# q and k of step 1 formed for two row tiles at once, and the memory pools of two layers laid over each other

## The chip, the core and the metric

The kernel runs on one core of a Trainium2 chip. The time is the device time of one execution in microseconds; before the change its median over three runs is 1698.4 us (1698.17 to 1698.85). The core has five engines that work side by side, each through its own queue in order: TensorE (PE in the profile, its weight loads PEld), VectorE (DVE), ScalarE (ACT), GpSimd (POOL) and SyncE (SP), which here only issues transfers.

## What is computed

The input is a feature matrix `x` (2708 x 256) and a weighted adjacency matrix `adj` (2708 x 2708). Layer 0 runs two steps of an attention with a nucleus cut beside a walk over the normalized adjacency:

```python
for n in range(2):
    q = Xa @ W1.T @ W2.T;  k = Xa @ W3.T          # 64 wide
    probs = softmax(q @ k.T)
    A = top_p(probs, 0.9), rows scaled to sum 1
    Xf = R @ Xf                                   # R = (adj + I) / row sums
    Xa = A @ Xa
    Z = Z + Xf @ U1[n].T + Xa @ U2[n].T
x = layernorm(x + layernorm(x + Z) * g + b)
```

Layer 1 is a graph attention with four heads over the nonzero entries of `adj`:

```python
Wh = x @ W[h]                                     # 64 wide, per head
e[i, j] = leaky_relu(s_i[i] + s_j[j], 0.2), masked by adj
out = layernorm(x + softmax_j(e) @ Wh)
```

## The kernel before

The 2708 rows are cut into 22 tiles: 16 of 128 rows and 6 of 110 (`rows`, `off`). Everything is float32.

**Layer 0** (`fast_layer0`, L454) has a setup that forms q and k of step 0 for groups of up to four tiles (L993 to L1014), and then two steps over the 22 row tiles (`step`, L947). For each row tile three kinds of work overlap:

- `search` (`scores`, then the cut): the logits of a tile three ahead (L594), their exponentials into `e` (L598), and then the nucleus threshold on DVE (L684 to L768), in step 1 with four passes of ACT (L619).
- `weigh` (L162): the attention. A tile's `e` is transposed by TensorE in six groups (L172), copied by ACT to `eT` (L178), and multiplied with the values (L187): `xe` in step 0, `ba` in step 1. After each group `between` runs one slot of other work.
- `walks` (L787): the product with the adjacency (L819), fed from SP's loads of `blk` (L93), a few matmuls for each slot.

When a walk or an attention of step 0 ends, a generator does the rest in pieces, one for each slot. `after_walk0` transposes the result by `turn` (L573, matmuls L577, copy L580) and multiplies it (`terms1`, L855); `after_attention0` (L841) transposes the attended tile `xa`, forms its q and k for step 1 in `project` (L559: four matmuls of 128 moving columns at L566, each shown as two records; copies L570 and L555 or L557), and multiplies it (`terms2`, L875), which yields `ba`. In step 1 `finish` adds the parts up on POOL (L894 to L896), does two layer norms by turns of DVE and POOL (L900 to L917), and calls `sources` (L136), which transposes the new `x` (L141), forms layer 1's values (L147, ACT to L157), stores them scaled to DRAM (`vd`, L160), and keeps three small factors (`sb`, `tj`, `s_src`).

Inside `with tc.manual_schedule` the order on PE, ACT, DVE and POOL is the order of the code. What lies outside it, layer 1 with it, is put between by a planner at build time, as its inputs and its memory come free by the planner's reckoning. SP's queue is ordered by the planner throughout.

At the end of layer 0 DVE sums up some flags of the cut, and a small matmul (L1078) adds them over the partitions.

**Layer 1** (`layer1`, L1090) goes over three groups of target tiles (8, 8 and 6) and, in each, over the 22 source tiles `j`. `targets` spreads `s_src` by transposes into `aux` (L1122) and ACT makes `r` of it (L1126). `neighbours` loads a block of `adjT` into `bar` (L1136; four buffers) and makes it a 0/1 mask (ACT L1137 and L1142; for diagonal blocks POOL L1140 and L1141 between). DVE makes four `pt` for each source tile (L1189, two buffers each), and TensorE sums them up: with the values `v` at L1197 and with `bj` for the denominators at L1204. Before the loop, ACT issues the loads of all 22 `v` (L1103) and POOL spreads all 22 `bj` (L1104). The function `settle` ends a group.

**Memory.** A pool takes a stretch of SBUF, pools lie one behind the other in the order in which they are opened, and layer 1's start again where layer 0's started. A tile of layer 1 can be written when the tiles of layer 0 on the same addresses have been read for the last time. The same holds for the eight banks of PSUM. Before the change layer 0's order is `w0`, `rowp`, `keep` (with `qT`, `yw`, `ba`, `rinv`, `kT1`), `heldp`, `sortp`, `finp`, `ep`, `wk`, `tpp`, `adjp`, and layer 1's is `keep1` (`v`, `bj`), `pp`, `rp`, `adjp1`, `pj`.

Of the kernel before, what the change touches and what calls it, by code (L numbers as in the profile page):

```python
# [8 lines left out]
F32 = mybir.dt.float32  # L9
# [5 lines left out]
PSUM = bass.MemoryType.PSUM  # L15

P = 128
# [21 lines left out]
HELD = 8  # L39
# [6 lines left out]
def kernel(  # L46
# [407 lines left out]
    def fast_layer0():  # L454

        l0 = ExitStack()
        w0 = l0.enter_context(tc.tile_pool(name="w0", bufs=1))
        rowp = l0.enter_context(tc.tile_pool(name="rowp", bufs=2))
        keep = l0.enter_context(tc.tile_pool(name="keep", bufs=1))
        HN = N // 2  # L460
        HT = NT // 2
        pieces = [(c, min(CHUNK, HN - c)) for c in range(0, HN, CHUNK)]
# [10 lines left out]
        heldp = l0.enter_context(tc.tile_pool(name="heldp", bufs=HELD))  # L473
# [40 lines left out]
        nc.gpsimd.memset(wants, 0.0)  # L514
        nc.gpsimd.memset(haves, 0.0)

        qT = keep.tile([P, N], F32, name="qT")
        yw = keep.tile([P, NT, D], F32, name="yw")
        ba = keep.tile([P, NT, D], F32, name="ba")
        rinv = keep.tile([P, NT], F32, name="rinv")  # L520

        dram = l0.enter_context(tc.tile_pool(name="dram", bufs=1, space=bass.MemoryType.DRAM))
        c1 = [dram.tile([P, D], F32, name=f"c1_{t}") for t in range(NT)]
        c2 = [dram.tile([P, D], F32, name=f"c2_{t}") for t in range(NT)]

        sortp = l0.enter_context(tc.tile_pool(name="sortp", bufs=1))
        finp = l0.enter_context(tc.tile_pool(name="finp", bufs=2))
        ep = l0.enter_context(tc.tile_pool(name="ep", bufs=3))
        wk = l0.enter_context(tc.tile_pool(name="wk", bufs=1))

        kT = [wk.tile([P, HN], F32, name="junk"), keep.tile([P, HN], F32, name="kT1")]
        tpp = l0.enter_context(tc.tile_pool(name="tpp", bufs=3))
        adjp = l0.enter_context(tc.tile_pool(name="adjp", bufs=3))
        ps_lg = l0.enter_context(tc.tile_pool(name="ps_lg", bufs=2, space=PSUM))
        ps_tr = l0.enter_context(tc.tile_pool(name="ps_tr", bufs=2, space=PSUM))
        ps_at = l0.enter_context(tc.tile_pool(name="ps_at", bufs=1, space=PSUM))
        ps_wk = l0.enter_context(tc.tile_pool(name="ps_wk", bufs=1, space=PSUM))


        tr = ps_tr.tile([P, 4, P], F32, name="tr")  # L540
# [15 lines left out]
            if low < m:  # L556
                copy(kT[s][DA:P, c0 + low - HN : c0 + m - HN], src[DA:P, low:m])  # L557

        def project(s, t, xT, copy_q, copy_k):  # L559

            m = rows[t]
            c0 = off[t]
            pj = ps_tr.tile([P, 4, P], F32, name="tr")
            for n, w in enumerate((wq, wk_sb)):
                for c in range(DC):
                    nc.tensor.matmul(  # L566
                        pj[:, n, :m], w[:, c].rearrange("p h e -> p (h e)"), xT[:, c, :m],
                        start=(c == 0), stop=(c == DC - 1),
                    )
            copy_q(qT[:, c0 : c0 + m], pj[:, 0, :m])  # L570
            keep_k(s, c0, m, pj[:, 1], copy_k)

        def turn(src, m, tp, copy):  # L573

            xT = rowp.tile([P, DC, P], F32, name="xT")
# [252 lines left out]
        def after_walk0(t, ac):  # L828
# [9 lines left out]
            terms1(t, xT)  # L838
            unfinished.remove(t)

        def after_attention0(t, xa):  # L841
            yield
            tp = ps_tr.tile([P, 4, P], F32, name="tr")
            xT = turn(xa, rows[t], tp, nc.scalar.copy)
            yield
            project(1, t, xT, nc.scalar.copy, nc.scalar.copy)
            yield
            terms2(t, xT)

        def terms1(t, xT):  # L850

            m = rows[t]
            cy = ps_tr.tile([P, 4, P], F32, name="tr").rearrange("p a b -> p (a b)")
            for c in range(DC):
                nc.tensor.matmul(  # L855
                    cy[:m], xT[:, c, :m], u_sb[:, 0, c].rearrange("p s e -> p (s e)"),
                    start=(c == 0), stop=(c == DC - 1),
                )
            r = rinv[:m, t : t + 1]
            cs = rowp.tile([P, D], F32, name="cs")  # L860
            nc.scalar.activation(cs[:m], cy[:m, 0:D], AF.Copy, scale=r)
            nc.scalar.activation(yw[:m, t, :], cy[:m, D : 2 * D], AF.Copy, scale=r)

            own = rowp.tile([P, D], F32, name="own")
            nc.gpsimd.tensor_scalar(own[:m], yw[:m, t, :], r, None, op0=ALU.mult)
            nc.gpsimd.tensor_add(cs[:m], cs[:m], own[:m])
            nc.gpsimd.tensor_add(cs[:m], cs[:m], xe[:m, t, 0:D])
            nc.gpsimd.dma_start(c1[t][:m], cs[:m])
# [78 lines left out]
        def step(s, cur, spend):  # L947
            for t in range(NT):
# [140 lines left out]

    def layer1():  # L1090
        l1 = ExitStack()
        keep = l1.enter_context(tc.tile_pool(name="keep1", bufs=1))
        pp = l1.enter_context(tc.tile_pool(name="pp", bufs=2))
        GT = 8
        spans = [list(range(g, min(g + GT, NT))) for g in range(0, NT, GT)]
        GW = GT * rows[0]


        v = [keep.tile([P, H, FO], F32, name=f"v{t}") for t in range(NT)]
        bj = [keep.tile([P, H, 32], F32, name=f"bj{t}") for t in range(NT)]  # L1100
        for t in range(NT):
            m = rows[t]
            nc.scalar.dma_start(v[t][:m].rearrange("p h o -> p (h o)"), vd[t][:m])  # L1103
# [4 lines left out]
        rp = l1.enter_context(tc.tile_pool(name="rp", bufs=2))  # L1108
        adjp = l1.enter_context(tc.tile_pool(name="adjp1", bufs=4))
        pj = l1.enter_context(tc.tile_pool(name="pj", bufs=2))  # L1110
        ps_v = l1.enter_context(tc.tile_pool(name="ps_v", bufs=1, space=PSUM))
        ps_u = l1.enter_context(tc.tile_pool(name="ps_u", bufs=2, space=PSUM))

        def targets(g):

# [55 lines left out]
        for g, span in enumerate(spans):  # L1171
# [6 lines left out]
            for j in range(NT):  # L1178
# [91 lines left out]
```

The softmax here doesn't subtract the row's maximum and nothing guards it: scores larger than these inputs give would overflow.

## Time and profile before

The profiled execution spans 1697.3 us. Busy time of the engines in stretches of it, in us:

| stretch | what runs | PE | DVE | ACT | POOL | clock of PE |
|---|---|---|---|---|---|---|
| 100 to 600 (500 us) | step 0 | 492.6 | 242.7 | 167.4 | 55.7 | 1.00 |
| 700 to 1200 (500 us) | step 1 | 494.8 | 460.1 | 331.2 | 206.7 | 1.00 |
| 1260 to 1310 (50 us) | end of layer 0, begin of layer 1 | 28.5 | 11.4 | 15.3 | 21.0 | 0.76 |
| 1400 to 1600 (200 us) | layer 1 | 196.4 | 174.2 | 71.6 | 44.6 | 1.00 |

A line of the groups gives line, engine, operation, output and input tiles and the number of instructions; then busy time, mean duration of one, and the idle time of the engine before them with what ended it. Matmuls of this engine are pipelined, so the durations of neighbours overlap, and the distance from start to start is shorter than a duration. A line of the timeline gives the start in us, the time that the merged run of instructions took, engine, line, operation and their number; a bracket tells how long the engine stood idle before it and who released it.

### The profile page before, as it was taken

Reading aid. Unit: us, or ns where it says so; the run is one execution under the profiler, and the core shown is the slowest. Engines: PE = TensorE matmul, PEld = TensorE weight load, DVE = VectorE, ACT = ScalarE, POOL = GpSimd, SP = SyncE. Lnnn points to the kernel's source line nnn. Section 1 sums busy time; section 2 is a strip of 40 time slices with the busy share of each in tenths; the row PEclk is TensorE's granted clock in tenths of the full one; section 3 lists DMA queues with packets and bytes.
Section 4 is the critical chain, followed back from the end, with each engine's and each line's share of the span. In section 5 each row is a group of like instructions: output and inputs, shape, how many; then the busy total and the mean of one; then the engine's idle time right before and its main releaser. Section 6 shows DMA issues by size and latency. Waiting matters only on the chain. (4 is left out here: it accounts for less than half of the span.)

```text
span 1697.3 us, 24178 instructions
## 1 busy us (share of the span) xinstructions
PE 1620.3 (95%) x8306; PEld 1064.8 (63%) x8306; DVE 1219.5 (72%) x3660; ACT 767.9 (45%) x1324; POOL 433.6 (26%) x915
## 2 busy tenths in 40 slices
PE   7999999999999999999999999999985999999895
PEld 4677777777767766777878788777773232322332
DVE  2954554556445029888899999998981989889886
ACT  1333333333333256566666767676723444243231
POOL 0310111111101033223344444453434200430312
PEclk9999999999999999999999999999996999999997
DMA  6211011101111133122223323322204323232231
GB/s 164 72 46 46 27 41 39 43 27 39 40 42 40 44 89 77 48 67 75 71 74 82 85 65 87 80 71 66 68 22 126 100 82 94 87 86 78 73 85 31
DMA packets 153873, 113.89 MB, mean 67 GB/s; under 512 B 39898, under 2 KB 144094, under 8 KB 153742
## 3 DMA queue, kind: packets, MB, share of 16 engines
q1 hardware_dynamic: 146248, 102.41, 22.7%
q0 software_dynamic: 2112, 5.55, 1.0%
q10 hardware_dynamic: 5382, 4.32, 0.9%
q8 instruction: 67, 1.10, 0.3%
q14 instruction: 64, 0.52, 0.1%
HBM read 101.16 MB, written 11.09 MB: 66 GB/s over the span
## 5 line engine op out<-in xcount | busy, mean ns | idle before, releaser
L1189 DVE SCALAR_TENSOR_TENSOR pt<-r,tj,bar 128x1024 f32<-128x1024 f32 (+3 forms) x264 | 297.0, 1187 | 49.8 <-ACT bar L1142 25.5
L619 ACT ACTIVATE junk<-e,minus,rth 128x2708 bf16<-128x2708 f32 (+1 forms) x88 | 233.0, 2648 | 36.1 <-POOL rth L651 35.3
L819 PE MATMUL walk<-xe,blk 128*128 128x257 f32 (+3 forms) x968 | 240.6, 382 | 0.0
L187 PE MATMUL att<-ba,eT 128*128 128x256 f32 (+3 forms) x968 | 234.4, 383 | 5.0 <-ACT eT L178 5.0
L187 PE MATMUL att<-xe,eT 128*128 128x256 f32 (+3 forms) x968 | 233.3, 381 | 4.3 <-ACT eT L178 4.3
L1197 PE MATMUL acc<-pt,v 128*64 128x512 f32 (+3 forms) x1056 | 230.5, 554 | 4.6 <-DVE pt L1189 4.6
L178 ACT COPY eT<-tr 128x512 f32<-128x512 f32 (+5 forms) x264 | 138.2, 538 | 203.3 <-PE tr L172 203.0
L819 PE MATMUL walk<-yw,blk 128*128 128x256 f32 (+3 forms) x968 | 228.0, 381 | 1.8 <-ACT xw L889 1.8
L699 DVE MAX8 cand<-e 128x8 f32<-128x170 f32 (+1 forms) x352 | 89.3, 324 | 171.5 <-ACT e L598 171.5
L819 PEld LDWEIGHTS walk<-xe,blk 128*128 128x128 f32 (+3 forms) x968 | 173.0, 186 | 53.1 <-issue 29.3
L819 PEld LDWEIGHTS walk<-yw,blk 128*128 128x128 f32 (+3 forms) x968 | 176.7, 186 | 41.6 <-issue 11.5
L187 PEld LDWEIGHTS att<-ba,eT 128*128 128x128 f32 (+3 forms) x968 | 171.9, 187 | 33.0 <-ACT eT L178 10.0
L187 PEld LDWEIGHTS att<-xe,eT 128*128 128x128 f32 (+3 forms) x968 | 170.8, 186 | 30.9 <-ACT eT L178 7.2
L598 ACT ACTIVATE e<-lg 128x1024 f32<-128x1024 f32 (+1 forms) x132 | 121.1, 922 | 132.3 <-PE lg L594 132.3
L1197 PEld LDWEIGHTS acc<-pt,v 128*64 128x64 f32 (+1 forms) x1056 | 73.7, 137 | 154.8 <-issue 111.9
L172 PE MATMUL tr<-ident,e 128*128 128x128 f32 (+3 forms) x968 | 140.5, 269 | 4.6 <-ACT xT L580 3.8
L172 PEld LDWEIGHTS tr<-ident,e 128*128 128x128 f32 (+3 forms) x968 | 115.0, 138 | 32.7 <-ACT xT L580 6.1
L1137 ACT ACTIVATE bar<-bar 128x1024 f32<-128x1024 f32 (+3 forms) x66 | 63.0, 956 | 146.0 <-DMA bar<-in_adjT_dram 110.1
L1204 PE MATMUL acc<-pt,bj 128*32 128x512 f32 (+3 forms) x1056 | 124.5, 549 | 0.0
L605 POOL TENSOR_TENSOR fact<-zp 128x1 f32<-128x1 f32 (+1 forms) x44 | 24.9, 566 | 329.2 <-ACT e L598 319.4
L699 DVE MAX8 cand<-scr 128x8 f32<-128x97 f32 (+1 forms) x616 | 101.9, 247 | 0.0
L832 DVE TENSOR_TENSOR xf<-walk,xe 128x257 f32<-128x257 f32 (+1 forms) x22 | 9.4, 427 | 117.4 <-PE walk L819 117.3
(199 smaller groups left out, 2022.1 us busy)
## 6 DMA issues: line engine op xcount, KB each, us to landing
blk<-in_adjT_dram SPq DMA_DIRECT2D x32, 704.0 KB
bar<-in_adjT_dram SPq DMA_DIRECT2D x32, 512.0 KB
blk<-in_adjT_dram SPq DMA_DIRECT2D x32, 330.0 KB
blk<-in_adjT_dram SPq DMA_DIRECT2D x32, 320.0 KB
blk<-in_adjT_dram SPq DMA_DIRECT2D x12, 605.0 KB
bar<-in_adjT_dram SPq DMA_DIRECT2D x12, 440.0 KB
bar<-in_adjT_dram SPq DMA_DIRECT2D x16, 330.0 KB
c<-cs POOLq DMA_DIRECT2D x32, 128.0 KB, 2.1
```

The costliest lines, as they stand in the source:

```text
L172: nc.tensor.transpose(tr[: rows[t], q, :m], e[:m, off[t] : off[t + 1]], ident[:m, :m])
L178: copy(eT[:k, : len(grp), :m], tr[:k, : len(grp), :m])
L187: nc.tensor.matmul(acc, eT[: rows[t], q, :m], value(t), start=(t == 0), stop=(t == NT - 1),)
L598: nc.scalar.activation(halves[:m, :, c0 : c0 + w], lg[:m, :, :w], AF.Exp, accum_out=zp[:m, n : n + 1],)
L605: nc.gpsimd.tensor_add(z, zp[:m, 0:1], zp[:m, 1:2])
L619: nc.scalar.activation(junk[:m], e[:m], func, scale=rth, bias=minus1[:m], accum_out=acc)
L699: nc.vector.max(cand[:, n, :], src[:m, n * size : min(N, (n + 1) * size)])
L819: nc.tensor.matmul(ac[:m, :w], blk[: rows[j], j - j0, :m], cur[: rows[j], j, 0:w], start=(j == 0), stop=(j == NT - 1),)
L1137: nc.scalar.activation(bar, bar, AF.Sign)
L1189: nc.vector.scalar_tensor_tensor(pt[:k, :gw], r[:k, h, :gw], tj[:k, j, h : h + 1], mask, op0=ALU.max, op1=ALU.mult,)
L1197: nc.tensor.matmul(acc[h // 2][c][q * FO : (q + 1) * FO, :w], v[j][:k, h - 1 + q, :], pts[h - 1 + q][:k, c0 : c0 + w], **at,)
L1204: nc.tensor.matmul(acc[2][c][h * 32 : (h + 1) * 32, :w], bj[j][:k, h, :], pts[h][:k, c0 : c0 + w], **at,)
```

## The change

Two things are changed. First, q and k of step 1 are formed once for two row tiles: the transposed tiles of a pair lie side by side in `xT2`, and `project` multiplies both with one set of matmuls of 256 moving columns (220 for the pairs of 110 rows). `xa` of step 0 then lies in `heldp`, and `own` has one buffer. Second, the pools of both layers are opened in an order in which each stretch of layer 1 lies over tiles of layer 0 that come free early enough for it; `v` and `bj` are allotted from the last tile to the first. With it the loads of `v` go from ACT's queue to SP's, and they and the copies of `bj` are written inside the first group's loop, one for each source tile.

```diff
     def fast_layer0():
 
         l0 = ExitStack()
-        w0 = l0.enter_context(tc.tile_pool(name="w0", bufs=1))
-        rowp = l0.enter_context(tc.tile_pool(name="rowp", bufs=2))
-        keep = l0.enter_context(tc.tile_pool(name="keep", bufs=1))
+
+        heldp, finp, rowp, w0, keep, sortp, adjp, ep, tpp, wk = (
+            l0.enter_context(tc.tile_pool(name=name, bufs=bufs))
+            for name, bufs in (
+                ("heldp", HELD), ("finp", 2), ("rowp", 2), ("w0", 1), ("keep", 1),
+                ("sortp", 1), ("adjp", 3), ("ep", 3), ("tpp", 3), ("wk", 1),
+            )
+        )
+        ps_lg, ps_wk, ps_at, ps_tr = (
+            l0.enter_context(tc.tile_pool(name=name, bufs=bufs, space=PSUM))
+            for name, bufs in (("ps_lg", 2), ("ps_wk", 1), ("ps_at", 1), ("ps_tr", 2))
+        )
...
-        qT = keep.tile([P, N], F32, name="qT")
         yw = keep.tile([P, NT, D], F32, name="yw")
         ba = keep.tile([P, NT, D], F32, name="ba")
         rinv = keep.tile([P, NT], F32, name="rinv")
+        qT = keep.tile([P, N], F32, name="qT")
...
-        def project(s, t, xT, copy_q, copy_k):
-
-            m = rows[t]
-            c0 = off[t]
-            pj = ps_tr.tile([P, 4, P], F32, name="tr")
-            for n, w in enumerate((wq, wk_sb)):
+        def project(s, c0, w, xT, copy_q, copy_k):
+
+            pj = ps_tr.tile([P, 4, P], F32, name="tr").rearrange("p (n a) b -> p n (a b)", n=2)
+            for n, wm in enumerate((wq, wk_sb)):
                 for c in range(DC):
                     nc.tensor.matmul(
-                        pj[:, n, :m], w[:, c].rearrange("p h e -> p (h e)"), xT[:, c, :m],
+                        pj[:, n, :w], wm[:, c].rearrange("p h e -> p (h e)"), xT[:, c, :w],
                         start=(c == 0), stop=(c == DC - 1),
                     )
-            copy_q(qT[:, c0 : c0 + m], pj[:, 0, :m])
-            keep_k(s, c0, m, pj[:, 1], copy_k)
+            copy_q(qT[:, c0 : c0 + w], pj[:, 0, :w])
+            keep_k(s, c0, w, pj[:, 1], copy_k)
...
+        pair = []
+
         def after_attention0(t, xa):
-            yield
+
+            m = rows[t]
+            yield
+            if t % 2 == 0:
+                pair[:] = [rowp.tile([P, DC, 2 * P], F32, name="xT2", bufs=1)]
+            both = pair[0]
+            xT = both[:, :, m * (t % 2) : m * (t % 2 + 1)]
             tp = ps_tr.tile([P, 4, P], F32, name="tr")
-            xT = turn(xa, rows[t], tp, nc.scalar.copy)
-            yield
-            project(1, t, xT, nc.scalar.copy, nc.scalar.copy)
-            yield
+            turn(xa, m, tp, nc.scalar.copy, xT)
+            yield
+            if t % 2:
+                project(1, off[t - 1], 2 * m, both, nc.scalar.copy, nc.scalar.copy)
+                yield
             terms2(t, xT)
...
-            own = rowp.tile([P, D], F32, name="own")
+            own = rowp.tile([P, D], F32, name="own", bufs=1)
...
-                        pool = heldp if s else rowp
-                        xa = pool.tile([P, D], F32, name=f"xa{s}")
+                        xa = heldp.tile([P, D], F32, name="xa1")
...
     def layer1():
         l1 = ExitStack()
-        keep = l1.enter_context(tc.tile_pool(name="keep1", bufs=1))
-        pp = l1.enter_context(tc.tile_pool(name="pp", bufs=2))
+
+        pp, keep, pj, adjp, rp = (
+            l1.enter_context(tc.tile_pool(name=name, bufs=bufs))
+            for name, bufs in (("pp", 2), ("keep1", 1), ("pj", 2), ("adjp1", 4), ("rp", 2))
+        )
+        ps_u = l1.enter_context(tc.tile_pool(name="ps_u", bufs=2, space=PSUM))
+        ps_v = l1.enter_context(tc.tile_pool(name="ps_v", bufs=1, space=PSUM))
...
-        v = [keep.tile([P, H, FO], F32, name=f"v{t}") for t in range(NT)]
-        bj = [keep.tile([P, H, 32], F32, name=f"bj{t}") for t in range(NT)]
-        for t in range(NT):
+        v, bj = {}, {}
+        for t in reversed(range(NT)):
+            v[t] = keep.tile([P, H, FO], F32, name=f"v{t}")
+            bj[t] = keep.tile([P, H, 32], F32, name=f"bj{t}")
+
+        def stationary(t):
             m = rows[t]
-            nc.scalar.dma_start(v[t][:m].rearrange("p h o -> p (h o)"), vd[t][:m])
+            nc.sync.dma_start(v[t][:m].rearrange("p h o -> p (h o)"), vd[t][:m])
             nc.gpsimd.tensor_copy(
                 bj[t][:m], sb[:m, t, :].unsqueeze(2).to_broadcast([m, H, 32])
             )
...
+                if g == 0:
+                    stationary(j)
                 mask = neighbours(g, j)
```

More of the change, by code (lines that the diff above doesn't have):

```diff
@@ L472, in fast_layer0 @@
         b_sb = w0.tile([P, D], F32, name="b_sb")
-        heldp = l0.enter_context(tc.tile_pool(name="heldp", bufs=HELD))
         tmp = heldp.tile([P, D], F32, name="xa1")
@@ L524, in fast_layer0 @@
         c2 = [dram.tile([P, D], F32, name=f"c2_{t}") for t in range(NT)]
[L526 to L529, printed above, removed]
         kT = [wk.tile([P, HN], F32, name="junk"), keep.tile([P, HN], F32, name="kT1")]
[L532 to L537, printed above, removed]
         tr = ps_tr.tile([P, 4, P], F32, name="tr")
@@ L557, in keep_k, with turn @@
                 copy(kT[s][DA:P, c0 + low - HN : c0 + m - HN], src[DA:P, low:m])
-        def project(s, t, xT, copy_q, copy_k):
-            m = rows[t]
-            c0 = off[t]
-            pj = ps_tr.tile([P, 4, P], F32, name="tr")
-            for n, w in enumerate((wq, wk_sb)):
+        def project(s, c0, w, xT, copy_q, copy_k):
+            pj = ps_tr.tile([P, 4, P], F32, name="tr").rearrange("p (n a) b -> p n (a b)", n=2)
+            for n, wm in enumerate((wq, wk_sb)):
                 for c in range(DC):
                     nc.tensor.matmul(
-                        pj[:, n, :m], w[:, c].rearrange("p h e -> p (h e)"), xT[:, c, :m],
+                        pj[:, n, :w], wm[:, c].rearrange("p h e -> p (h e)"), xT[:, c, :w],
                         start=(c == 0), stop=(c == DC - 1),
                     )
-            copy_q(qT[:, c0 : c0 + m], pj[:, 0, :m])
-            keep_k(s, c0, m, pj[:, 1], copy_k)
-        def turn(src, m, tp, copy):
-            xT = rowp.tile([P, DC, P], F32, name="xT")
+            copy_q(qT[:, c0 : c0 + w], pj[:, 0, :w])
+            keep_k(s, c0, w, pj[:, 1], copy_k)
+        def turn(src, m, tp, copy, xT=None):
+            if xT is None:
+                xT = rowp.tile([P, DC, P], F32, name="xT")
             for c in range(DC):
@@ L1106, in layer1 @@
             )
[L1108 to L1112, printed above, removed]
         def targets(g):
```

## The prediction

> **What bounds the kernel now.** I read the page's busy table and slices first, then the table by stage around the one weak slice, then the timeline there, and last the TensorE timeline inside step 1's projection. The chain that ended last is no help: it covers only the last 1.4 us.
>
> The busy table and the slices (each digit is a fortieth of the span, 42.4 us):
>
> ```profile
> PE 1620.3 (95%) x8306; PEld 1064.8 (63%) x8306; DVE 1219.5 (72%) x3660; ACT 767.9 (45%) x1324; POOL 433.6 (26%) x915
> PE   7999999999999999999999999999985999999895
> PEclk9999999999999999999999999999996999999997
> ```
>
> TensorE is the bound nearly everywhere. The one hole is where its row has 8 and 5 (about 1230 to 1315 us), the seam between the layers; the clock falls to 0.6 there. The table by stage cuts it finer:
>
> ```profile
> core 0: us, PE busy (x) PEld busy (x) DVE busy (x) ACT busy (x) POOL busy (x), PEclk, DMA share, GB/s
> 1279.70:1290.00 10.30, 4.91 (x21) 2.99 (x19) 3.13 (x9) 2.19 (x10) 7.97 (x14) 0.82 0.04 11
> 1290.00:1297.00 7.00, 6.13 (x23) 4.50 (x22) 0.33 (x1) 5.54 (x21) 0.00 (x0) 0.53 0.72 196
> 1297.00:1312.00 15.00, 3.17 (x17) 2.39 (x16) 1.31 (x2) 4.33 (x7) 6.46 (x25) 0.60 0.76 250
> 1312.00:1320.65 8.65, 8.62 (x32) 3.10 (x32) 8.65 (x7) 4.73 (x7) 6.12 (x6) 0.71 0.22 61
> 1320.65:1326.09 5.44, 5.44 (x36) 1.48 (x32) 5.44 (x5) 3.46 (x4) 1.79 (x2) 1.00 0.34 96
> ```
>
> The last attention matmul of layer 0 ends at 1279.7. Then comes the tail (residual sum, two layer norms and `sources` of the last tiles), an almost empty stretch, a slow first source tile of layer 1, and from 1320.65 the steady pace of 5.44 us per source tile. The timeline names the holder of the empty stretch:
>
> ```profile
> 1297.18 0.33 ACTq L1103 DMA_DIRECT2D v<-v  x1
> 1297.36 0.60 ACT L1126 ACTIVATE r<-aux 128x512 f32<-128x512 f32 x1
> 1297.55 11.04 ACTq L1103 DMA_DIRECT2D v<-v  x21
> 1308.63 1.09 ACT L1126 ACTIVATE r<-aux 128x512 f32<-128x512 f32 x2 [10.67 <-DMA v<-v]
> 1309.60 1.06 ACT L1142 ACTIVATE bar<-bar 128x1024 f32<-128x1024 f32 x1
> ```
>
> ACT issues all 22 loads of `v` while the rest of `r` and the first mask stand behind them in its queue; DVE's first `pt` starts at 1310.69 after 20.4 us of waiting for that mask, and TensorE's first `acc` at 1312.03.
>
> Inside step 0, the timeline of TensorE around one projection:
>
> ```profile
> 340.22 1.03 PE L819 MATMUL walk<-xe,blk 128*128 128x257 f32 x4
> 341.09 0.60 PE L172 MATMUL tr<-ident,e 128*128 128x128 f32 x4
> ...
> 343.26 0.61 PE L566 MATMUL tr<-xT,wq 128*128 128x128 f32 x4
> 343.71 0.61 PE L566 MATMUL tr<-xT,wk_sb 128*128 128x128 f32 x4
> 344.15 1.03 PE L819 MATMUL walk<-xe,blk 128*128 128x257 f32 x4
> ```
>
> Start to start is what counts here, not the duration: four records with 128 columns take 343.71 - 343.26 = 0.45 us, or 0.111 each; four with 257 take 341.09 - 340.22 = 0.87, or 0.218 each. The durations, 275 and 382 ns, overlap and would mislead.
>
> **What the Trainium skill says.** "TensorE: Matmul & The Clock Gate", section "Back-to-back issue gap", lets the gap of isolated matmuls grow with the moving columns plus a small constant, and warns that weight loads raise it at small widths. The trace shows proportion: 0.111 against 0.218, so no weight load shows at 128. The same page, "What's actually happening", says that an idle array falls to half rate and needs sustained work to recover; the trace agrees (clock 0.53 to 0.82 in the seam, four L147 records 2.10 us there against 1.05 at 1276). "DMA: Bandwidth & Descriptors", "Issuing engines are not separate DMA queues", says that the choice of issuing engine saves only sequencer time, usually small; here it is not small, 11.4 us of ACT. "GPSIMD Engine Reference", "Key points", says that GpSimd shares its SBUF interfaces with VectorE and contends with its instructions of two SBUF inputs; the trace agrees (L1141 takes 0.45 us before the first `pt` and 1.32 beside it).
>
> **The change, part by part.**
>
> Paired projection. Removed: 22 x 8 records of 128 columns at 0.111 us, or 16 for a pair, 1.78 us. Added: 8 of 256 at 0.218, 1.74 us. Saving 0.04 us a pair, 0.4 us over 11 pairs. The busy sums would have promised more (152 ns of busy a record against about 245, some 5 us in all), and I don't take them. ACT's copies of q and k become fewer and wider; ACT is 34% busy in step 0. The second tile of a pair now has all the projection in one slot: behind it in TensorE's queue stand walk matmuls (0.87 us) and transposes into the other of the two `tr` buffers, so I expect no new wait. The single `xT2` is last read some four slots before it is written again; the single `own` is touched by POOL alone, in order. `xa` of step 0 in `heldp`: eight buffers, no wait. I take 0.4 us, bounds -2 to +5.
>
> Loads of `v` on SP, one with each source tile. ACT loses 22 issues, 11.4 us, all on the path. SP gains 22 issues at about 0.35 us (its other issues there) in 120 us: hidden. Behind a waiting `v` load in SP's queue stand the `bar` loads; four of these are buffered, so a wait of some 16 us is covered. The copies of `bj` (POOL, 22 at 0.35 = 7.7 us) spread over 22 x 5.44 us, of which POOL has the larger part free.
>
> Pools laid over each other. I add up declared sizes in the order of opening. Before, `r` lay over `ba`, which the last attention still reads, and `bar` over `heldp`; the trace confirms it (SP's first `bar` waits 7.0 us for L909, which frees `hh`, and starts at 1290.40). After, offsets in KB: `heldp`, `finp`, `rowp` to 27.1; `w0` to 41.4; `yw` to 63.4; `ba` to 85.4; `qT`, `kT1` to 101.4; `sortp` to 104.1; `adjp` to 120.6; three `e` to 152.3. Layer 1: `pp` to 28.0, `v` and `bj` to 61.0 (tile 0 highest, over `yw`), `pt` to 93.0 (over `ba` and `qT`), `bar` to 109.0 (over `qT`, `kT1`, `sortp`, `adjp`), first `r` to 125.0 (over `adjp` and one `e`). So `bar` 0 and 1 can load once the last logits are done (1213), 2 and 3, `r` and `v` 0 to 12 by 1261, when the last walk matmul ends. `pt` waits for `ba`, until 1279.7. In PSUM `aux` now lies over `lg`, free from 1214; the first sums over `lg`, `walk` and `att`; the sums of `bj` (L1204) over `tr`, which the last `sources` holds until 1294.9.
>
> So masks and `r` can be ready when attention ends. DVE then makes 8 `pt` (tiles 0 and 1) at 1.3 to 1.47 us, 10.4 to 11.8 us, while the tail runs, and TensorE does their two L1197 groups of 3.65 us. L1204 of tile 0 waits for the tail. The tail, 15.2 us now, gets shorter by 1 us through a warmer clock and longer through sharing: four turns of DVE each behind up to one `pt` (0.7 us on average, 2.8), POOL's 5.3 us slowed by about half (2.6). End 1279.7 + 19.6 = 1299.3. The 8 x 8 `aux` records (8 tiles at 0.89 = 7.1 us) move from the empty stretch to before it; 3.3 us of that fit where TensorE stands at L1078, the rest, 3.8, delays all: 1303.1. Then L1204 of tile 0 (1.92) frees a `pt`, two new ones take 2.9, and tile 2 starts at about 1307.9; before, it starts at 1320.65 + 5.44 = 1326.09. Gain 18.2. The sharing costs assume that every turn of DVE meets a `pt` and that POOL never runs alone; I take a third of their 5.4 off again, 1.8, which gives 20. For the diagonal tiles 2 to 7 DVE at 5.3 to 5.9 us a tile can fall behind TensorE's 5.44 and cost up to 2.5; that I leave to the range. Bounds of the seam: at most, TensorE always busy from 1260 to 1326: 66.1 us hold 13.5 of attention, 7.1 of `aux`, about 4 of `sources` and 10.9 of tiles 0 and 1, 35.5, so 30 saved; at least, only the issue, 11.
>
> Sum: 1698.4 - 0.4 - 20 = 1678.
>
> **The rivals.** Full overlap: the tail is not slowed, `aux` fits in gaps; the gain nears its ceiling of 30, say 27, 1671. For it: TensorE idles 4.6 us in the tail before one L141. Against: L1204's wait for `tr`, and DVE is in both chains.
>
> Only the issue: the order on the queues is fixed in advance, and the new early work lands where its inputs come late; the 11.4 us of issue come back and little else: 1687. For it: L1078 stalls TensorE 3.3 us by just such a placement. Against: space is free 18 us earlier.
>
> Slower: 8 masks' passes and 8 `r` of about 1 us on ACT go ahead of attention's `eT` copies in the last 50 us (16 us of TensorE waits), and DVE at 5.9 stays above 5.44 for all 22 tiles (10 us), against 20 gained: 1704. For it: `att` already waits for `eT` 34 times, `pt` runs close to TensorE. Against: those waits are short (0.4 at most), `pt` means 1.33, 5.3 a tile, and step 1 leaves ACT a third free.
>
> **How the numbers follow.** Forecast 0.70, full overlap 0.12, only the issue 0.12, slower 0.06. Around the forecast the unsure terms (tail 4, order 4, projection 3) give about 1672 to 1684; the full case and most of the issue case reach from 1669 to 1687, which leaves about 0.15 out. Every case but the last is faster by more than 0.2%; a thin overlap between issue and slower gives "same" 0.02.
>
> **What would show it.** Right: L566 has half its records at 0.218 us a step, and step 0 ends within a microsecond or two of before; `bar` loads and `aux` before 1280; first `acc` near 1284 to 1290; L1204 of tile 0 at the end of the tail; afterwards 5.44 per tile. Wrong: step 0 shorter by 5 us (the busy sums were right), a `bar` or `v` wait of TensorE in the first group, `eT` waits grown before 1280, or L1204 not tied to the tail.

## The result, and the profile after

The changed kernel takes 1686.3 us (median of 4 runs, 1685.7 to 1686.9) against 1698.4 us before; the ratio is 0.9928, with a 95% interval of 0.9911 to 0.9945. It gained 12.1 us; the forecast was 20.4. The measured time is the one that the rival "only the issue" gave (1687). The edits move line numbers: `pt` L1189 is now L1198, the products with `v` L1197 are L1206, those with `bj` L1204 are L1213, the `bar` load L1136 is L1143, its passes L1137 and L1142 are L1144 and L1149, `v` L1103 is L1116, `bj` L1104 is L1117, `aux` and `r` L1122 and L1126 are L1129 and L1133, the layer norm's L909 is L915, the projection L566 is L562.

The page of the kernel after, its busy table, its TensorE row and its clock row:

```profile
PE 1615.3 (96%) x8218; PEld 1060.6 (63%) x8218; DVE 1222.5 (73%) x3660; ACT 764.2 (45%) x1302; POOL 432.0 (26%) x915
PE   7999999999999999999999999999997999999895
PEclk9999999999999999999999999999998999999998
```

The 88 TensorE records fewer are the paired projection. The slice that had 5 at a clock of 0.6 has 7 at 0.8. So the seam is shorter, not gone. The same table by stage as before, of the kernel after, cut at the end of attention, at the first `acc` and at the second and third source tile (duration, then busy time and count of PE, PEld, DVE, ACT and POOL, granted clock, DMA):

```profile
core 0: us, PE busy (x) PEld busy (x) DVE busy (x) ACT busy (x) POOL busy (x), PEclk, DMA share, GB/s
1277.60:1287.00 9.40, 4.96 (x28) 4.11 (x27) 3.04 (x8) 4.78 (x15) 7.98 (x16) 0.87 0.41 138
1287.00:1299.50 12.50, 7.21 (x28) 5.34 (x26) 5.30 (x3) 6.86 (x22) 6.39 (x24) 0.69 0.53 153
1299.50:1307.52 8.02, 7.96 (x33) 1.98 (x33) 8.02 (x7) 4.55 (x6) 5.67 (x6) 1.00 0.79 241
1307.52:1313.01 5.49, 5.49 (x36) 1.62 (x33) 5.49 (x6) 3.00 (x3) 2.27 (x3) 1.00 0.69 210
```

Attention ends at 1277.6 instead of 1279.7; the third source tile (tile 2) starts at 1313.01 instead of 1326.09, 13.1 us earlier; from there on it is 5.44 us a tile as before. TensorE's empty stretch of 12 us is gone, but 9.7 us of idle remain in the 21.9 us between the end of attention and the first `acc`. The timeline of that stretch:

```profile
1277.84 0.84 SPq L1143 DMA_DIRECT2D bar<-in_adjT_dram  x2
...
1284.89 0.63 PE L141 MATMUL tr<-ident,xe 110*128 110x110 f32 x2 [4.38 <-DVE xe L915]
1285.52 1.28 SPq L1116 DMA_DIRECT2D v<-v  x3
...
1286.15 1.72 POOL L1117 COPY bj<-sb 128x128 f32<-128x128 f32 x7
...
1288.87 4.03 DVE L915 TENSOR_SCALAR xe<-hh,ln_mv,ln_rs 110x256 f32<-110x256 f32 x1 [1.98 <-POOL ln_rs L912]
...
1290.75 2.00 POOL L1117 COPY bj<-sb 128x128 f32<-128x128 f32 x8
1293.04 0.60 PE L141 MATMUL tr<-ident,xe 110*128 110x110 f32 x2 [4.61 <-DVE xe L915]
...
1297.51 0.61 ACT L1133 ACTIVATE r<-aux 128x512 f32<-128x512 f32 x1
...
1298.22 10.86 DVE L1198 SCALAR_TENSOR_TENSOR pt<-r,tj,bar 128x1024 f32<-128x1024 f32 x8 [5.33 <-ACT r L1133]
1299.56 3.33 PE L1206 MATMUL acc<-pt,v 128*64 128x512 f32 x8 [0.74 <-DVE pt L1198]
```

Three things are to be seen. The first `bar` load is sent when attention has ended, not 17 to 65 us earlier, and `v` nearly 8 us after that. The copies of `bj` stand in runs in the middle of the tail, and beside them one L915 takes 4.03 us where the same instruction takes 0.41 us elsewhere. The first `pt` waits for `r`, whose last part comes out behind the tail's last transposes.

The pairing in step 0, from TensorE's timeline of the kernel after, a pair of 128 rows and one of 110:

```profile
124.56 1.02 PE L562 MATMUL tr<-xT,wq 128*128 128x256 f32 x4
125.43 1.03 PE L562 MATMUL tr<-xT,wk_sb 128*128 128x256 f32 x4
126.29 1.03 PE L816 MATMUL walk<-xe,blk 128*128 128x257 f32 x4
...
554.92 0.90 PE L562 MATMUL tr<-xT,wq 128*128 128x220 f32 x4
555.67 0.91 PE L562 MATMUL tr<-xT,wk_sb 128*128 128x220 f32 x4
556.41 1.03 PE L816 MATMUL walk<-xe,blk 128*128 128x257 f32 x4
```

A tile of 110 rows in the kernel before, for comparison:

```profile
557.53 0.59 PE L566 MATMUL tr<-xT,wq 128*128 128x110 f32 x4
557.96 0.61 PE L566 MATMUL tr<-xT,wk_sb 128*128 128x110 f32 x4
558.41 1.05 PE L819 MATMUL walk<-xe,blk 128*128 128x257 f32 x4
```

Start to start, the pair of 256 columns takes 1.73 us (before, twice 0.89), the pair of 220 columns 1.49 us (before, twice 0.88: with 110 columns a record took as long as with 128).

### The profile page after: what moved, and what is told of

Its sections match the earlier page's. It is cut to its first block, busy times and chain, and to the rows that moved or that the text cites. A ratio compares the mean times of both kernels' runs of the same rounds, so it can differ in the third digit from the quotient of the medians.

```text
span 1683.6 us, 23972 instructions
## 1 busy us (share of the span) xinstructions
PE 1615.3 (96%) x8218; PEld 1060.6 (63%) x8218; DVE 1222.5 (73%) x3660; ACT 764.2 (45%) x1302; POOL 432.0 (26%) x915
## 5 line engine op out<-in xcount | busy, mean ns | idle before, releaser
L1198 DVE SCALAR_TENSOR_TENSOR pt<-r,tj,bar 128x1024 f32<-128x1024 f32 (+3 forms) x264 | 297.0, 1186 | 33.8 <-issue 15.5
L187 PE MATMUL att<-ba,eT 128*128 128x256 f32 (+3 forms) x968 | 234.4, 384 | 4.8 <-ACT eT L178 4.8
L187 PE MATMUL att<-xe,eT 128*128 128x256 f32 (+3 forms) x968 | 233.3, 381 | 4.3 <-ACT eT L178 4.3
L1206 PE MATMUL acc<-pt,v 128*64 128x512 f32 (+3 forms) x1056 | 229.4, 549 | 4.6 <-DVE pt L1198 4.6
L187 PEld LDWEIGHTS att<-ba,eT 128*128 128x128 f32 (+3 forms) x968 | 171.9, 187 | 32.8 <-ACT eT L178 9.9
L187 PEld LDWEIGHTS att<-xe,eT 128*128 128x128 f32 (+3 forms) x968 | 170.9, 186 | 30.9 <-ACT eT L178 7.2
L1206 PEld LDWEIGHTS acc<-pt,v 128*64 128x64 f32 (+1 forms) x1056 | 72.8, 136 | 153.5 <-issue 111.3
L1144 ACT ACTIVATE bar<-bar 128x1024 f32<-128x1024 f32 (+3 forms) x66 | 62.9, 956 | 144.2 <-DMA bar<-in_adjT_dram 125.7
L1213 PE MATMUL acc<-pt,bj 128*32 128x512 f32 (+3 forms) x1056 | 124.7, 548 | 0.0
```

Of the source, the lines that this page charges most:

```text
L187: nc.tensor.matmul(acc, eT[: rows[t], q, :m], value(t), start=(t == 0), stop=(t == NT - 1),)
L1144: nc.scalar.activation(bar, bar, AF.Sign)
L1198: nc.vector.scalar_tensor_tensor(pt[:k, :gw], r[:k, h, :gw], tj[:k, j, h : h + 1], mask, op0=ALU.max, op1=ALU.mult,)
L1206: nc.tensor.matmul(acc[h // 2][c][q * FO : (q + 1) * FO, :w], v[j][:k, h - 1 + q, :], pts[h - 1 + q][:k, c0 : c0 + w], **at,)
L1213: nc.tensor.matmul(acc[2][c][h * 32 : (h + 1) * 32, :w], bj[j][:k, h, :], pts[h][:k, c0 : c0 + w], **at,)
```

## The experiments

All are timed against the kernel before on the same chip. "Tile 2" is the start of the third source tile's first product with `v`, the mark at which the seam is over; in the kernel before it is 1326.09.

| run | what it is | us | ratio, 95% interval | first `pt` | tile 2 |
|---|---|---|---|---|---|
| after | the change | 1686.3 | 0.9928 (0.9911 to 0.9945) | 1298.22 | 1313.01 |
| pair_only | before, with the pairing | 1695.4 | 0.9982 (0.9976 to 0.9989) | 1308.44 | 1323.12 |
| issue_only | before, with `v` on SP and `v`, `bj` in the loop | 1690.4 | 0.9956 (0.9940 to 0.9973) | 1299.37 | 1317.57 |
| pools_only | after, without the pairing | 1687.2 | 0.9937 (0.9921 to 0.9954) | 1295.29 | 1313.94 |
| bj_act | after, with `bj` copied by ACT | 1682.1 | 0.9904 (0.9888 to 0.9921) | 1294.20 | 1310.12 |
| split_act | bj_act, with finer pools in layer 0 | 1683.3 | 0.9913 (0.9896 to 0.9929) | 1296.54 | 1311.12 |
| early | split_act, with pools in the order of release | 1682.0 | 0.9904 (0.9887 to 0.9920) | 1295.77 | 1310.34 |
| r_first | early, with `r` written into the last attention tiles | 1689.9 | 0.9952 (0.9935 to 0.9968) | 1283.21 | 1315.02 |
| r_tail | the same, with `r` right behind attention | 1682.5 | 0.9908 (0.9892 to 0.9925) | 1290.21 | 1308.43 |
| r_tail_b | r_tail, with masks that load late | 1683.5 | 0.9913 (0.9896 to 0.9929) | 1290.62 | 1309.44 |

My theory after the result was: a pool of layer 1 waits until every *pool* of layer 0 that it lies over is wholly released, so adding up addresses tile by tile promised too much; and the copies of `bj` hurt the tail. The rivals were release tile by tile, and that only the loads' issue on ACT had ever mattered.

### The pairing alone

```diff
-            project(1, t, xT, nc.scalar.copy, nc.scalar.copy)
+            if t % 2:
+                project(1, off[t - 1], 2 * m, both, nc.scalar.copy, nc.scalar.copy)
```

> The kernel before with the paired projection alone. If a record's cost is its start-to-start distance, 256 columns save 0.04 us for each of 8 pairs and 220 columns some 0.27 for each of 3 (a 110-column record keeps the 0.108 us of a 128-column one): 1.1 us, up to 2 with small waits, so about 1697. If the busy sums are the cost: 5 us, 1693. The seam between the layers stays as it was: first L1189 31 us after the last attention matmul.

It gained 2.8 us, a little more than the 1.1 to 2 expected. The timeline around the seam:

```profile
1278.10 0.35 PE L141 MATMUL tr<-ident,xe 110*128 110x110 f32 x2
...
1295.90 10.44 ACTq L1110 DMA_DIRECT2D v<-v  x22
...
1308.44 4.08 DVE L1196 SCALAR_TENSOR_TENSOR pt<-r,tj,bar 128x1024 f32<-128x1024 f32 x3 [19.71 <-ACT bar L1149]
```

The end of attention comes 1.6 us earlier. By the start-to-start times the records save 8 pairs x 0.05 + 3 pairs x 0.27 = 1.2 us, so most of the 1.6 is accounted for; a shift of 0.5 us comes without any pairing too (issue_only ends attention at 1279.15, the kernel before at 1279.67). The rest of the gain is in the seam, where the 22 issues take 10.4 instead of 11.4 us and tile 2 is 3.0 us earlier; why that part came with the pairing I did not settle.

### The issue alone

```diff
-        for t in range(NT):
+        def stationary(t):
             m = rows[t]
-            nc.scalar.dma_start(v[t][:m].rearrange("p h o -> p (h o)"), vd[t][:m])
+            nc.sync.dma_start(v[t][:m].rearrange("p h o -> p (h o)"), vd[t][:m])
...
+                if g == 0:
+                    stationary(j)
```

> The kernel before with only the loads of v on SP and v and bj written inside the first group's loop; order of pools as before. If what the changed kernel gained at the seam is the 11.4 us of issue on ACT: about 1687, first pt near 1299. If the new order of pools brought most of it: 1692 or more, since v then waits for the last store of the tail and r for the last layer norm.

It gained 7.8 us, and 1690.4 us lies between the two expected sums. The timeline of the kernel with the issue moved:

```profile
1297.15 5.25 POOL L1104 COPY bj<-sb 128x128 f32<-128x128 f32 x22
...
1299.37 8.72 DVE L1191 SCALAR_TENSOR_TENSOR pt<-r,tj,bar 128x1024 f32<-128x1024 f32 x4 [9.59 <-DMA bar<-in_adjT_dram]
...
1304.00 1.81 PE L1206 MATMUL acc<-pt,bj 128*32 128x512 f32 x2 [4.03 <-DVE pt L1191]
```

The first `pt` of the kernel before:

```profile
1310.69 31.61 DVE L1189 SCALAR_TENSOR_TENSOR pt<-r,tj,bar 128x1024 f32<-128x1024 f32 x24 [20.37 <-ACT bar L1142]
```

The first `pt` comes 11.3 us earlier (1310.69 to 1299.37), which is the 11.4 us of issue that the prediction read in the trace before. But although each copy of `bj` is written at its own source tile, POOL runs all 22 in one go right behind its first mask operations (L1140 and L1141, the second at 1296.75), and beside that run one of four `pt` takes 4.53 us. The four take 8.72 us; in the kernel before 24 of them ran in 31.61 us there, or 5.3 for four. So 3.4 us are lost again, and 11.3 less 3.4 is 7.9, about the 7.8 measured.

### The pools without the pairing

```diff
-            if t % 2:
-                project(1, off[t - 1], 2 * m, both, nc.scalar.copy, nc.scalar.copy)
+            project(1, t, xT, nc.scalar.copy, nc.scalar.copy)
```

> The changed kernel with the projection of one tile at a time again, all else kept. If the two parts are independent: 1.1 to 2 us above the changed kernel, 1687.4 to 1688.3. If the pairing also helped the seam: above 1690.

It gained 10.9 us. The timeline of this kernel:

```profile
1290.35 0.59 PE L141 MATMUL tr<-ident,xe 110*128 110x110 f32 x2
1295.29 9.15 DVE L1191 SCALAR_TENSOR_TENSOR pt<-r,tj,bar 128x1024 f32<-128x1024 f32 x7 [5.09 <-DMA v<-cs]
...
1298.23 3.74 POOL L1110 COPY bj<-sb 128x128 f32<-128x128 f32 x3
1299.57 3.58 PE L1206 MATMUL acc<-pt,bj 128*32 128x512 f32 x12 [3.68 <-POOL bj L1110]
```

Here `bj` comes behind the tail, not into it, and the tail's last L141 is 10.9 us after the end of attention (1279.4). Now the other side waits: three copies take 3.74 us beside `pt` (in the kernel after, eight took 2.00), and TensorE stands 3.68 us for one. The gains of this kernel (10.9) and of the pairing alone (2.8) add up to 13.7 and not to 12.1; the intervals do not tell these apart. What the traces do show is that the order planned ahead for each kernel puts the same copies into a different place.

This kernel has the issue on SP too. Beside issue_only, timed in the same series, it tells what the new order of the pools is worth: 3.1 us (1690.4 against 1687.2; the intervals of the ratios overlap, the single runs, 1690.3 to 1691.4 and 1686.9 to 1688.2, do not). Both have copies of `bj` beside `pt`.

### The copies of `bj` on ACT

```diff
-            nc.gpsimd.tensor_copy(
+            nc.scalar.copy(
                 bj[t][:m], sb[:m, t, :].unsqueeze(2).to_broadcast([m, H, 32])
             )
```

> The changed kernel with the 22 copies of bj on ACT in place of POOL. If these copies stretch the tail (POOL queue, and DVE's last layer-norm step of 4.03 us beside them): that step back at 0.4 to 0.8 us, the last L141 4 to 5 us earlier after the attention's end, and 1681.5 to 1683. If the tail does not set when layer 1 starts, because r is made in an order fixed in advance: no change, 1686.

It is 16.0 us faster than before and, by the two ratios, about 4.1 us faster than the change (the two intervals just overlap; the single runs, 1680.9 to 1683.0 and 1685.7 to 1686.9, do not). Its timeline:

```profile
1278.65 0.84 SPq L1143 DMA_DIRECT2D bar<-in_adjT_dram  x2
...
1286.32 1.28 SPq L1116 DMA_DIRECT2D v<-v  x3
...
1288.68 0.41 DVE L915 TENSOR_SCALAR xe<-hh,ln_mv,ln_rs 110x256 f32<-110x256 f32 x1 [1.00 <-POOL ln_rs L912]
...
1289.24 0.38 PE L141 MATMUL tr<-ident,xe 110*128 110x110 f32 x2
...
1294.20 4.08 DVE L1198 SCALAR_TENSOR_TENSOR pt<-r,tj,bar 128x1024 f32<-128x1024 f32 x3 [5.10 <-DMA v<-cs]
```

L915 is back at 0.41 us, the last L141 stands 10.8 us behind the end of attention instead of 15.4, and the first `pt` is 4.0 us earlier (its bracket names a store; the last part of `r` ends 0.1 us before it, at 1294.09). Of these 4.0 us, 2.9 are left at tile 2, and the profiled span is 3.0 us shorter. That the copies on POOL stretched the tail is thus shown, by taking them away; their price is 3 to 4 us.

### Finer pools

```diff
-        heldp, finp, rowp, w0, keep, sortp, adjp, ep, tpp, wk = (
+        heldp, finp, rowp, w0, ywp, bap, keep, sortp, adjp, ep, tpp, wk, gbp = (
...
-        yw = keep.tile([P, NT, D], F32, name="yw")
-        ba = keep.tile([P, NT, D], F32, name="ba")
+        yw = ywp.tile([P, NT, D], F32, name="yw")
+        ba = bap.tile([P, NT, D], F32, name="ba")
```

(`g_sb` and `b_sb` go from `w0` to `gbp` likewise.)

> The run before it (bj copies on ACT) with one more edit: in step 1's memory plan yw, ba and the pair g_sb/b_sb get pools of their own, so that v of layer 1 no longer lies over a pool that holds something which the tail reads. Tile addresses stay nearly the same. Theory (a new pool waits for every whole pool that it lies over): the v loads, first at 1286.3 us there, come right behind the first bar load, by 1277 to 1281; the first bar load stays within 2 us of 1278.6, because its issue stands behind a store of the tail on SP. Rival (release tile by tile): nothing moves, v stays at 1286 or later. On either theory the first pt still waits for r, at 1293 to 1295, so the time is 1681 to 1683.

The timeline of the kernel with finer pools, in which lines past the pools are 11 higher (the `bar` load is L1154, `v` L1127, `pt` L1209):

```profile
1259.33 0.36 SPq L1154 DMA_DIRECT2D bar<-in_adjT_dram  x1
1264.05 0.82 SPq L1127 DMA_DIRECT2D v<-v  x2
...
1296.54 3.68 DVE L1209 SCALAR_TENSOR_TENSOR pt<-r,tj,bar 128x1024 f32<-128x1024 f32 x3 [5.48 <-ACT r L1144]
```

The loads moved by 19 us (`bar`) and 22 us (`v`), with the tiles at nearly the same addresses; only the borders of the pools are new. Release tile by tile is out. SP's waits name readers that fit: the first `bar` is released by L906, the last to read `rinv`, which lies in `keep`, and goes out 0.03 us after it ends; the first `v`, that of tile 0, is released after 4.3 us by L1094, the last to read `ones`, which lies in `w0`. By the sums of addresses `bar` does not lie over `rinv`, nor `v` of tile 0 over `w0`. I was wrong in one point: I had held `bar` to stay where it was, behind a store on SP; the order there is planned anew, and it went ahead of that store, with `v` behind it. And the time did not fall: the first `pt` still waits for `r`, and comes 2.3 us later than in bj_act.

### Pools in the order of release

```diff
-        heldp, finp, rowp, w0, ywp, bap, keep, sortp, adjp, ep, tpp, wk, gbp = (
+        heldp, finp, rowp, ywp, keep, adjp, sortp, wk, w0, ep, bap, tpp, gbp = (
...
-        pp, keep, pj, adjp, rp = (
+        pp, rp0, adjp, pj, keep, rp1 = (
```

(The sums of `bj` get a PSUM pool of their own as well.)

> All of that, and the pools of step 1 stand in the order in which they come free (the r buffers in two pools, so that the first lies over what is dead long before attention ends; the bj sums in a PSUM pool of their own over the tail's buffer alone). Theory (whole pools set the earliest start, but the order on the queues is a second limit): first r and bar at 1258 to 1278, v by 1281; the transposes for r stand between the tail's in PE's order, so the first pt comes at 1291 to 1295 and the time is 1679 to 1682. Rival (memory alone holds layer 1 back): first pt soon after 1280 and a time of 1670 to 1675.

The first `bar` is sent at 1259.71 and the first part of `r` comes at 1265.05, and the first `pt` at 1295.77 all the same: 1682.0 us, as bj_act. Memory alone does not hold layer 1 back. TensorE's timeline shows what holds `r` (`aux` is L1143 here):

```profile
1282.29 1.04 PE L1143 MATMUL aux<-ident,s_src 128*128 128x128 f32 x8
1288.10 0.63 PE L141 MATMUL tr<-ident,xe 110*128 110x110 f32 x2 [4.78 <-DVE xe L926]
1288.53 0.63 PE L1143 MATMUL aux<-ident,s_src 128*128 128x128 f32 x2
...
1293.91 1.04 PE L1143 MATMUL aux<-ident,s_src 128*128 128x128 f32 x8
```

The `aux` blocks stand behind the tail's L141 in TensorE's queue, and so wait for the layer norm with it.

### `r` written into attention, and behind it

`yw` gets a place of its own that lives through both layers, the first `r` is a view of it, and the transposes go through the logit banks:

```diff
+        def first_targets():
+            r = r_over_yw()
+            for t in range(0, GT, 2):
+                lg = ps_lg.tile([P, 2, CHUNK], F32, name="lg")
...
-                if next(stream, True):
-                    break
+                more = next(stream, None)
+                if more is None:
+                    next(early, None)
+                if more is None or more:
+                    break
```

> The run named early with one more edit: the 64 transposes for r of the first group and their 8 exponentials are written by hand into the last tiles of step 1's attention, after the last random-walk tile, through the two idle logit banks of PSUM and into the memory of yw, which is dead by then. Theory (with the loads early, the place of r behind the tail's transposes is what holds layer 1 back): r is whole at about 1278, the first pt comes at 1279 to 1283 instead of 1295.8, the first acc before 1286, among the tail's work, and the time falls by 7 to 13 us against early, to 1669 to 1675. Rival (the tail itself, its DVE and POOL chain of some 11 us, is the end of the seam whatever lies beside it): pt and acc come earlier but the third tile's acc does not by more than 3 us, and the time stays at 1679 or more.

1689.9 us. The theory's 1669 to 1675 is out. The rival's open end, 1679 or more, holds the time, but it did not foresee a loss: against early it is 7.8 us slower, and tile 2 comes 4.7 us later. (The first group needs 8 x 4 = 32 transposes; the 64 of this expectation and the next is a miscount.) The timeline of this kernel (`aux` is L960, `r` L963 into `yw`, the bar passes L1188 and L1193, `eT` L182, the tail's transposes L145, `pt` L1245):

```profile
1271.84 1.05 ACT L1188 ACTIVATE bar<-bar 128x1024 f32<-128x1024 f32 x1
1271.99 0.65 PE L960 MATMUL lg<-ident,s_src 128*128 128x128 f32 x4 [1.34 <-ACT yw L963]
...
1283.21 3.68 DVE L1245 SCALAR_TENSOR_TENSOR pt<-yw,tj,bar 128x1024 f32<-128x1024 f32 x3 [17.54 <-DMA v<-cs]
...
1285.10 0.35 PE L145 MATMUL tr<-ident,xe 110*128 110x110 f32 x2
...
1291.72 1.80 POOL L929 TENSOR_TENSOR ln_rs<-ln_ve,minus_half 110x1 f32<-110x1 f32 x1
...
1308.60 2.10 PE L151 MATMUL tr<-wx,xT 128*110 128x264 f32 x4 [4.08 <-ACT xT L147]
```

The first `pt` is indeed 12.6 us earlier than in early. But attention ends at 1285.1 instead of 1279.9, because the `aux` blocks wait for ACT (4.4 us in four places), which has masks and `eT` copies in the same queue, and the attention products stand behind the waiting `aux`. And the tail's POOL and DVE turns meet `pt` (L929 1.80 instead of 0.57 us). The longest of these meetings is a mask operation of POOL, L1192: 5.16 us beside four `pt` in a row, instead of 0.45. A mask pass of ACT (L1193) waits 7.2 us for it, and behind that pass in ACT's queue stands the copy L147 of the tail. So the tail's last product, L151, starts 23.5 us after the end of attention, and products of layer 1 wait behind it. Tile 2 starts at 1315.02.

> The run r_first with the hand-placed block moved: all 64 transposes and 8 exponentials for r stand right behind the last attention product, where PE waits 4.4 us for xe anyway. Theory (r_first lost its gain twice: r and the masks between the eT copies on ACT made the last two tiles of attention 6 to 7 us longer, and the pt beside the tail's DVE and POOL work made the tail some 5 us longer): attention ends within 2 us of the run early (1280), r is whole and the first pt comes at 1286 to 1289, the tail ends at 1293 to 1297, and the time is 1676 to 1682. Rival (any layer 1 work beside the tail costs as much as it gains): 1683 to 1690.

With the same block right behind attention (only the place of the call differs) it is 1682.5 us, between the two expected ranges, and no faster than early or bj_act (1682.0 and 1682.1). TensorE's timeline, where L1250 is the product with `v`, L1257 with `bj`, L151 the tail's product:

```profile
1289.18 0.35 PE L145 MATMUL tr<-ident,xe 110*128 110x110 f32 x2
1291.60 3.07 PE L1250 MATMUL acc<-pt,v 128*64 128x512 f32 x4 [2.07 <-issue]
1294.60 1.63 PE L151 MATMUL tr<-wx,xT 128*110 128x264 f32 x4
1296.06 0.35 PE L145 MATMUL tr<-ident,xe 110*128 110x110 f32 x2
```

Layer 1 now begins inside the tail, and tile 2 starts at 1308.43, the earliest of all runs and next to the prediction's 1307.9. The theory's numbers are off in three places: the first `pt` is at 1290.21 instead of 1286 to 1289, the tail's last product starts at 1299.06 where its end was expected at 1293 to 1297, and the time stands just above the expected upper end. The tail's last L145 is 16.6 us behind the end of attention, because products of layer 1 are in front of it in the queue. Against early, tile 2 gained 1.9 us and the time nothing; in this the rival, that work beside the tail costs what it gains, was nearer. Of the 17.7 us by which tile 2 is earlier than in the kernel before, the profiled spans keep 17.0 and the medians 15.7; the difference I did not follow.

> The same with the mask pool put last in layer 1's plan, over memory that comes free at the end of attention, so that no mask stands between the eT copies on ACT. Theory: attention ends 1 to 2 us earlier than in r_tail, at about 1278; the masks then compete with the exponentials for ACT in the tail, and the first pt comes at 1286 to 1290; time 1675 to 1682. Rival: masks that come late hold the pt of tiles 1 to 3 back and the time is above that of r_tail by 2 us or more.

```diff
-        pp, adjp, pj, keep, rp1 = (
+        pp, pj, keep, rp1, adjp = (
```

Attention ends 1.9 us earlier than in r_tail (1277.5 against 1279.4), so masks between the `eT` copies cost about that. The masks come late in turn, the first `pt` is no earlier (1290.62), and 1683.5 us is above the theory's 1675 to 1682 and 1 us more than in r_tail, less than the rival's 2. The two differences cancel within what the intervals tell.

## Why the prediction was right and wrong

Its direction was right and its sum was too large by 8.3 us: 1686.3 lies outside the 1672 to 1684 that it gave around its own forecast, and inside its whole range only because a rival's case was counted in. By its own steps:

**Paired projection, 0.4 us: too small.** The price of 0.05 us for a pair of 128 rows was right. The working took the same price for the six tiles of 110 rows, whose records I had not read; with 0.27 for each of their three pairs the records give 1.2 us. Alone the pairing measured 2.8. That the busy sums (5 us) would mislead was right, and the end of step 0 came forward by some 2 us as asked.

**Loads of `v` on SP, 11.4 us all on the path: right.** Alone it brought the first `pt` 11.3 us forward. But "the copies of `bj` spread over 22 x 5.44 us, of which POOL has the larger part free" was wrong. Work that is written late in a loop runs when its inputs and its place in the queue allow, here in runs within 11 us, inside the tail (after) or beside the first `pt` (issue_only). It cost 3 to 4 us in either place. This is the first mis-sized term: priced at nothing, measured 3 to 4.

**Pools: the step that failed.** By the prediction's sum they had to bring some 9 us beyond the 11 of the issue; pools_only is 3.1 us faster than issue_only. "I add up declared sizes", and "`bar` 0 and 1 can load once the last logits are done (1213), 2 and 3, `r` and `v` 0 to 12 by 1261" let each tile wait for the tile under it, as the section on the kernel before also puts it. What counts is the last reader of every pool underneath. `bar` lay over `keep`, which also holds `ba`, and `ba` is read until attention ends: first load 1277.84. `v` and `bj` lay over `w0`, which also holds `b_sb`, and the tail reads `b_sb`: first load 1285.52, after a wait of 4.2 us that L922, the last to add `b_sb`, ends. The trace of before does not tell: its first `v` load, at 1297.18, comes 2.3 us after the tail's last store, from a `rowp` tile, but ACT, in whose queue it stands, had work up to then. The run with finer pools shows it, 19 and 22 us for moving borders. The PSUM part of the working fits: the first `aux` ran at 1234.77, before the change at 1280.40.

**"So masks and `r` can be ready when attention ends": a second failure behind the first.** With the loads at 1259 and 1264 (split_act) nothing was gained. The order on the queues is fixed in advance, and `r` stands behind L141, which waits for the layer norm. That was the ground of the rival "only the issue", and the rival was right in it; its sum, 11.4 us, comes near by accident, since issue alone gives 7.8, the pairing some, the pools the rest. Where `r` was written at the end of attention by hand, the first `pt` came 5.6 us earlier than in early, so the place of `r` did hold it back; but the time stayed at 1682.5, so this place alone did not set it. There tile 2 came at 1308.4, near the predicted 1307.9, but by another way: the first `pt` stood at 1290.2, where the prediction has it when attention ends (1279.7), and products of layer 1 stretched the tail. Whether the sum's working of the overlap (tail, DVE turns, `aux` in front) holds, no run shows. One count in it is wrong: the `aux` of eight tiles are 8 x 4 records, not 8 x 8. Their price, 0.89 us a tile, was read where the clock stood at 0.53; in early, at 1280.11, eight records (two tiles) took 1.04 us.

**The 1.8 us taken off again, and the tail of 19.6 us.** The tail took 20.0 us (1277.6 to about 1297.6, when ACT has read the last `tr`), the predicted length by luck: it came through `bj` and not through `pt`, which began only afterwards. That L1213 of tile 0 is tied to the end of the tail can't be told apart in the kernel after, since L1206 is too.

**What was asked of the profile.** Right: half the records in L562, step 0 within 2 us, `eT` waits not grown (4.8 us for L187 on `ba`, before 5.0), 5.44 us a tile afterwards. "`bar` loads and `aux` before 1280" came true by the letter, with `aux` from 1234.77 and the first two `bar` loads at 1277.84; but these went out 0.2 us after attention had ended, not ahead of it as the working has it. Wrong: the first `acc` at 1299.56 instead of 1284 to 1290. "Full overlap" and "slower" did not come; the mechanism of "slower", layer 1's work on ACT between `eT` copies, did come in r_first.

The seam's term in numbers: tile 2 was predicted at 1307.9. It came at 1313.0, with `bj` off POOL at 1310.1, and with `r` by hand as well at 1308.4.

## What to carry to other kernels

When pools lie over each other, look up the last reader of each whole pool underneath, not of the tile at the same address, and put tiles with late readers into pools of their own. Then ask what is second in line: here loads 20 us earlier brought nothing. The transposes for `r` stood in TensorE's queue behind others that waited, and moving these by hand brought the first `pt` forward, but not the end. Small copies "on an idle engine" are not free if that engine and the one on the path keep each other out; find out when they will run before you price them at nothing.

## What was unexpected of the hardware

One L915, a one-source fp32 operation of VectorE, took 4.03 us beside a run of GpSimd copies and ended 0.15 us after the run did (1292.90 and 1292.75); without them it took 0.41. The Trainium skill, "SBUF — State Buffer", section "Who interferes with whom", says that VectorE in a two-port mode and GpSimd contend for a shared pair of ports, that whoever issues first holds it for the whole instruction, and that `tensor_scalar` can enter such a mode. The trace agrees with the blocking; but one copy takes 0.25 us, and the wait lasted about a dozen of them and two mask operations (1288.9 to 1292.75), so GpSimd's next instruction seems to have got ahead of the waiting one each time. Which instructions were in that mode no run shows. It goes the other way too: copies beside `pt` took 1.25 us each (3.74 for three in pools_only) instead of 0.25, and L1192 in r_first, 5.16 us, ended 0.3 us after the last of four `pt` in a row (1307.03 and 1306.72).

A matmul record with 110 moving columns took as long as one with 128 (0.11 us start to start), while 220 and 256 columns took 0.187 and 0.218. So joining two tiles of 110 rows saved more (0.27 us) than joining two of 128 (0.05).
